# Wq and Wk as four loads of 128 whole rows, and pair 0's exponentials in two other rooms

## The chip, the cores and the metric

The kernel runs on one core of one Trainium2 chip. The metric is the device time of one execution in microseconds (us). A core has a matrix engine (PE), whose weight loads are listed as PEld, a vector engine (DVE), a scalar engine (ACT), a general engine (POOL) and a synchronizing engine (SP). Each engine runs its own list of instructions strictly in the listed order and waits at an instruction until all that it needs is there. DMA transfers are issued by SP, ACT or POOL and are carried by 16 DMA engines that all three share.

## The reference

There are 128 graphs of 128 nodes with 512 features, all in float32, and two layers:

```python
# layer 0, for each graph
h = relu(layernorm(x))
Xw = h @ Wv + bv;  sj = Xw @ aw[:512];  si = Xw @ aw[512:]
alpha = adj * exp(leaky_relu(sj[None, :] + si[:, None] + ab, 0.2))
T = alpha / (alpha.sum(-1) + 1e-12)
x = x + relu(sum over k of (T^k h) @ Wk[k] + bk[k])        # k = 0, 1, 2
# layer 1
h = relu(layernorm(x))
q, k = split(h @ Wqk);  v = h @ Wv1                        # Wqk is 512 x 1024
w = mask / sqrt(512) * rowsum(q * (adj @ (k * mask)))
x = x + softmax(w over the nodes)[:, None] * v
```

## The kernel before

The graphs are taken in 64 pairs. Both layers' products with weights are done by Strassen's scheme on 2 x 2 blocks: seven block products in place of eight, for which sums of blocks are made beforehand, of the weights once (`combine`, L205 to L211) and of the activations for each pair (`left_sums`, L407 to L410). Layer 0's weights are read as blocks b11, b12, b21, b22 (1536 columns each: three powers k), and their four sums stand in the tile `tw`, 4 x 1536 columns. Line 421 holds nearly all of PE's work.

The main loop over pairs (L596) is preceded by a setup (L557 to L588), and everything that the diff touches is in that setup:

- `norm0(0)` makes h of pair 0 and writes it to DRAM (`hd`, L310) and back in another layout (`hv`, L314), from which two DVE transposes (L320, one for each graph j of the pair) make h transposed in the tile X[0].
- `wv0_sums` multiplies the four row chunks of Wv (L133, loaded by SP) with the attention vector (L160, DVE). `attention_weights` spreads the result over the partitions by PE (L122) into `u_bc` (L168, ACT). `score_sums` (L303, DVE) then makes pair 0's scores, and `attention(0)` makes T: sums z (L353), leaky relu (L354), exponential (L356, ACT), products with the adjacency and row sums (L359), division (L361 to L365).
- `score_matrix(o)`, o = 0 to 3, makes Wq Wk^T, chunk by chunk of 128 columns of Wq and of Wk. For each o there are eight PE transposes (L236), two ACT copies (L239, L241) and the matmuls that add up in four banks (L247). Chunks 0 and 1 are loaded on ACT's queue at the start. Chunks 2 and 3 are loaded on POOL's queue into the buffers of chunks 0 and 1, so POOL waits there until PE has transposed these. A load takes 128 columns of all 512 rows, in runs of 512 bytes.
- POOL's queue also carries the blocks b for k = 1 and 2 (L202). The first of these is held behind the landing of Wv's chunk 0 by a one-column copy (L199).
- `t_transposed(0)`, `begin(0)` (the two transposes L320), `propagate(0)` (T h and T^2 h by PE, L400, copied by ACT, L402), `prepare0(0)` (the sums L407 to L410) and `combine` (L207 to L210) end the setup, followed by pair 1's norm and score sums.

The source order is not the order that the engines run. When the program is built, a scheduler takes for each engine the earliest instruction in the source that, by its own estimates of durations and of transfers, is ready. If none of a step's instructions is ready, it takes a later one. So the lists are fixed before the run. Where a tile is reused, or a region of a tile is written again, the scheduler adds the dependency, region by region. In the kernel before, z and the exponentials of pair 0 lie in `tw`, in 256 columns across the border of its first two quarters, so `combine`'s sums L207 and L209, which write these quarters, must come after T.

A transfer on SP's or ACT's queue also waits until an earlier transfer that used the same one of a few completion counters has landed.

Of the kernel before, what the change touches and what calls it, by code (L numbers as in the profile page):

```python
# [8 lines left out]
FP = mybir.dt.float32  # L9
AF = mybir.ActivationFunctionType  # L10
OP = mybir.AluOpType
# [4 lines left out]
def kernel(  # L16
# [20 lines left out]
    nc = tc.nc  # L37
    B, N, D = x.shape
    K = wk.shape[0]
    P = 128  # L40
    DC = D // P
    HC = DC // 2
    HD = D // 2
    G = 2
# [6 lines left out]
    const = ctx.enter_context(tc.tile_pool(name="const", bufs=1))  # L51
    loads = ctx.enter_context(tc.tile_pool(name="loads", bufs=3))
    front = ctx.enter_context(tc.tile_pool(name="front", bufs=2))
# [12 lines left out]
    xg, ag, agb = {}, {}, {}  # L66

    def load(p):
        load_x(p)
        load_agb(p)  # L70

    def load_x(p):
        s = slice(p * G, (p + 1) * G)
        xg[p] = loads.tile([P, G, D], FP, name="xg")
        nc.sync.dma_start(xg[p], x[s].rearrange("b n d -> n b d"))
        if p > 0:
            load_ag(p)

    def load_ag(p):
        s = slice(p * G, (p + 1) * G)  # L80
        ag[p] = loads.tile([P, G, N], FP, name="ag")
        nc.sync.dma_start(ag[p], adj[s].rearrange("b n m -> n b m"))
# [13 lines left out]


    load_x(0)
    e01 = setup.tile([P, HC, 2, HD], FP, name="e01")
    nm = setup.tile([B, N], FP, name="nm")  # L100
# [3 lines left out]
    wpool = setup_ctx.enter_context(tc.tile_pool(name="wpool", bufs=2))  # L104
    b12 = setup.tile([P, K, HC, HD], FP, name="b12")

    f = [const.tile([P, HC, 2, HD], FP, name=f"f{i}") for i in range(1, 5)]
# [5 lines left out]
    ident = const.tile([P, P], FP, name="ident")  # L113
# [7 lines left out]

        nc.tensor.transpose(dst, col.to_broadcast([P, P]), ident)  # L122

    def wqk_chunk(a, o, queue):
        w = wpool.tile([P, DC, P], FP, name=f"w{a}")
        at = a * D + o * P
        queue.dma_start(w, wqk[:, at:at + P].rearrange("(c p) o -> p c o", p=P))
        return w

    nc.scalar.dma_start(awr, aw.rearrange("n o -> o n"))  # L130
    wchunks = {0: [wqk_chunk(a, 0, nc.scalar) for a in range(2)]}
    for c in range(DC):
        nc.sync.dma_start(wv0_sb[c], wv0[c * P:(c + 1) * P])  # L133
    load_ag(0)
# [3 lines left out]
    bsum = const.tile([P, D], FP, name="bsum")  # L138
    nc.gpsimd.dma_start(bsum[:K], bk)
    nc.gpsimd.dma_start(nm, nodemask)  # L140
    wchunks[1] = [wqk_chunk(a, 1, nc.scalar) for a in range(2)]


    u_bc = const.tile([P, 2, D], FP, name="u_bc")
# [48 lines left out]
    def block0(pool, name, kh, nh):  # L193


        t = b12 if pool is None else pool.tile([P, K, HC, HD], FP, name=name)
        rows(t[:, 0], wk[0, :, nh * HD:(nh + 1) * HD], kh)
        if kh == nh == 0:
            nc.gpsimd.tensor_copy(t[:, 1, 0, 0:1], wv0_sb[0][:, 0:1])  # L199
        for k in range(1, K):  # L200
            src = wk[k, kh * HD:(kh + 1) * HD, nh * HD:(nh + 1) * HD]
            nc.gpsimd.dma_start(t[:, k], src.rearrange("(c p) o -> p c o", p=P))  # L202
        return t
# [23 lines left out]
    def score_matrix(o):  # L227

        if o == 0:
            pms.extend(ps_m.tile([P, D], FP, name="pm") for _ in range(DC))  # L230
        ws = wchunks.pop(o)
        wt = []
        for a in range(2):
            p = ps_t.tile([P, DC, P], FP, name="pt")
            for c in range(DC):
                nc.tensor.transpose(p[:, c, :], ws[a][:, c, :], ident)  # L236
            t = wpool.tile([P, D], FP, name=f"wt{a}")
            if a:
                nc.scalar.copy(t, p.rearrange("p c i -> p (c i)"))  # L239
            else:  # L240
                nc.scalar.copy(t.rearrange("p (f c a) -> p f c a", f=Q, c=DC),  # L241
                               p.rearrange("p c (f a) -> p f c a", f=Q))
            wt.append(t)
        if o + 2 < DC:
            wchunks[o + 2] = [wqk_chunk(a, o + 2, nc.gpsimd) for a in range(2)]
        for c in range(DC):
            nc.tensor.matmul(pms[c], wt[0][:, c * P:(c + 1) * P], wt[1],  # L247
                             start=(o == 0), stop=(o == DC - 1))
            if o == DC - 1:
                for nh in range(2):  # L250
                    nc.scalar.copy(e[c // HC, nh][:, c % HC, 0, :], pms[c][:, nh * HD:(nh + 1) * HD])
# [35 lines left out]
    H, HV, S, PZ, X, SX, AT, T, TT, X1, H2, X2, SX2 = ({} for _ in range(13))  # L287
# [29 lines left out]
    def transposed(hv, dst):  # L317

        for j in range(G):
            nc.vector.transpose(dst[:, j].rearrange("p f (n b) -> p f n b", n=Q),  # L320
                                hv[:, j].rearrange("p n (f a) -> p f n a", f=Q))
# [23 lines left out]
            spread(pz[:, j, :], col[:, j:j + 1])  # L345
        return pz[:, :G]

    def attention(p, room):

        a, s, pz = ag.pop(p), S.pop(p), PZ.pop(p)  # L350
        z = room.rearrange("p (g n) -> p g n", g=G)
        for j in range(G):
            nc.vector.tensor_scalar(z[:, j, :], pz[:, j, :], s[:, G + j:G + j + 1], cz, op0=OP.add, op1=OP.add)  # L353
        nc.vector.scalar_tensor_tensor(z, z, 0.2, z, op0=OP.mult, op1=OP.max)  # L354
        ex = z
        nc.scalar.activation(ex, z, AF.Exp)  # L356
        d = small.tile([P, 2, G], FP, name="d")
        for j in range(G):
            nc.vector.scalar_tensor_tensor(ex[:, j, :], ex[:, j, :], 1.0, a[:, j, :], op0=OP.mult,  # L359
                                           op1=OP.mult, accum_out=d[:, 0, j:j + 1])  # L360
        nc.vector.tensor_scalar(d[:, 0], d[:, 0], 1e-12, None, op0=OP.add)  # L361
        nc.vector.reciprocal(d[:, 1], d[:, 0])
        t = T[p] = front.tile([P, G, N], FP, name="t", bufs=1)
        for j in range(G):
            nc.vector.tensor_scalar(t[:, j, :], ex[:, j, :], d[:, 1, j:j + 1], None, op0=OP.mult)  # L365

        if p > 0:
            transposed_adj(p)

    def transposed_adj(p):  # L370

        AT[p] = front.tile([P, G, N], FP, name="aT", bufs=3)
        nc.vector.transpose(AT[p].rearrange("p g n -> p (g n)"),
                            agb.pop(p).rearrange("p g q i -> p (g q i)"))
        for j in range(G):
            b = p * G + j
            nc.scalar.activation(AT[p][:, j, :], AT[p][:, j, :], AF.Copy, scale=maskT[:, b:b + 1])

    def t_transposed(p):

        t, tt = T.pop(p), front.tile([P, G, 2, N], FP, name="tt", bufs=1)
        pt = ps_t.tile([P, DC, P], FP, name="pt")
        for j in range(G):
            nc.tensor.transpose(pt[:, j, :], t[:, j, :], ident)  # L384
        nc.scalar.copy(tt[:, :, 0, :], pt[:, :G, :])
        pt = ps_t.tile([P, DC, P], FP, name="pt")
        for j in range(G):
            nc.tensor.matmul(pt[:, j, :], t[:, j, :], tt[:, j, 0, :], start=True, stop=True)  # L388
        nc.scalar.copy(tt[:, :, 1, :], pt[:, :G, :])  # L389
        TT[p] = tt  # L390

    def propagate(p):

        h, tt = H.pop(p), TT.pop(p)
        for j in range(G):
            for kh in range(2):
                pt = ps_t.tile([P, HC, 2, N], FP, name="pt")
                for c in range(HC):
                    at = (kh * HC + c) * P
                    nc.tensor.matmul(pt[:, c].rearrange("p k n -> p (k n)"), h[:, j, at:at + P],  # L400
                                     tt[:, j].rearrange("p k n -> p (k n)"), start=True, stop=True)
                nc.scalar.copy(X[p][:, 1:3, j, kh].rearrange("p k c n -> p c k n"), pt)  # L402
# [150 lines left out]
    def begin(p):  # L553
        X[p] = front.tile([P, K, G, 2, HC, N], FP, name="x")
        transposed(HV.pop(p), X[p][:, 0].rearrange("p j h c n -> p j (h c) n"))

    norm0(0)  # L557
    wv0_sums()
    score_matrix(0)
    blocks0["b11"] = block0(const, "b11", 0, 0)  # L560
    score_matrix(1)
    attention_weights()
    masks()
    score_sums(0)
    blocks0["b12"] = block0(None, "b12", 0, 1)
    blocks0["b22"] = block0(const, "b22", 1, 1)
    load_x(1)
    blocks0["b21"] = block0(const, "b21", 1, 0)
    score_matrix(2)

    tw = const.tile([P, 4, K, HC, HD], FP, name="t")
    at = K * HC * HD - N
    attention(0, tw.rearrange("p i k c o -> p (i k c o)")[:, at:at + G * N])
    score_matrix(3)
    bias()
    t_transposed(0)
    begin(0)
    propagate(0)
    prepare0(0)
    right0.update(combine(t=[tw[:, i] for i in (0, 2, 1, 3)], **blocks0))  # L580
# [15 lines left out]
    for p in range(NP + 1):  # L596
        if p < NP:
            if p + 1 < NP:
                n = p + 1
# [19 lines left out]
        elif p > 0:  # L619
            yv, w = strassen1(p - 1, p + 2)  # L620
# [6 lines left out]
        if p < NP:  # L627
# [4 lines left out]
            else:  # L632
                transposed_by_pe(H2[p], hT2)
            a = {(j, kh): X2[p][:, j, kh:kh + 1].rearrange("p k c n -> p k (c n)")
                 for j in range(G) for kh in range(2)}
# [26 lines left out]
```

## Time and profile before

| | us |
|---|---|
| median of 6 runs | 2367.32 (2364.67 to 2370.24) |
| the profiled execution's own time | 2369.57 |
| its span on the core | 2367.8 |
| PE busy | 2341.6 (99%) |
| DVE busy | 1824.9 (77%) |
| ACT busy | 638.0 (27%) |
| POOL busy | 380.3 (16%) |

A line of the timeline gives the start, the busy time, the engine and source line, the operation, what it writes and reads, and in brackets the idle time of the engine before it with what ended it. A line of the waits gives who waited for what, then total time, count and the longest wait. A line of the windows gives a stretch of the span, its length, the busy time of each engine in it, the share of PE's full clock that was granted, the DMA share and GB/s.

### The profile page before, as it was taken

How to read it: one execution, taken by the hardware profiler on the slowest of the kernel's cores; microseconds unless marked ns; L12 is line 12 of the kernel's file. 1: busy time of each engine (PE TensorE's matmuls, PEld its weight loads, DVE VectorE, ACT ScalarE, POOL GpSimd, SP SyncE). 2: the span in 40 equal slices, each digit the busy share in tenths (PEclk: the TensorE clock that was granted, in tenths of full speed). 3: DMA queues.
4: the chain of work that ended last, by engine and by line, in shares of the span. 5: the costliest groups of instructions: out<-in, count | busy, mean ns of one | idle time of the engine just before them, and what ended most of it. 6: DMA issues, size and time to landing. Idle time of an engine off the chain costs nothing.

```text
span 2367.8 us, 27872 instructions
## 1 busy us (share of the span) xinstructions
PE 2341.6 (99%) x8929; PEld 1660.4 (70%) x8929; DVE 1824.9 (77%) x4959; ACT 638.0 (27%) x1562; POOL 380.3 (16%) x662
## 2 busy tenths in 40 slices
PE   7999999999999999999999999999999999999998
PEld 4677676676776776776766767767767667667675
DVE  6787877877877778878778778778787787787775
ACT  3222222322222222223223222222222232232221
POOL 4111111111111111111111111111111111111100
PEclk9999999999999999999999999999999999999999
DMA  7234344244343343343442443433434434424321
GB/s 209 88 97 107 97 108 106 82 117 111 85 116 106 91 107 101 104 107 89 117 106 82 116 111 86 116 104 93 107 101 104 107 89 116 107 81 116 105 63 49
DMA packets 253670, 242.88 MB, mean 103 GB/s; under 512 B 28318, under 2 KB 178846, under 8 KB 253522
## 3 DMA queue, kind: packets, MB, share of 16 engines
q1 hardware_dynamic: 228096, 211.87, 31.5%
q0 software_dynamic: 23312, 28.18, 6.4%
q8 instruction: 70, 1.15, 0.2%
q10 hardware_dynamic: 2114, 1.05, 0.2%
q14 instruction: 78, 0.64, 0.1%
HBM read 140.72 MB, written 100.27 MB: 102 GB/s over the span
## 4 chain that ended last, share of the span: by engine, by line
PE 90%; DVE 3%; DMA 2%; issue 1%; ACT 0%; POOL 0%; DVEq 0%; POOLq 0%
PE pm L421 76%; PE pt L400 8%; PE pt L519 4%; PE pt L388 1%; DMA pwd<-pwt 1%; PE pt L384 1%; DMA pw<-pwd 0%; DVE st L260 0%; DMA pz<-pzd 0%; DMA pzd<-pzt 0%; DVE x L549 0%; DVE x L461 0%; DVE x L320 0%; DVE junk L303 0%; DVE sx L409 0%
## 5 line engine op out<-in xcount | busy, mean ns | idle before, releaser
L421 PE MATMUL pm<-t,sx 128*128 128x256 f32 x2304 | 508.0, 379 | 2.9 <-DVE sx L408 2.9
L421 PEld LDWEIGHTS pm<-t,sx 128*128 128x128 f32 x2304 | 437.5, 190 | 63.0 <-DVE sx L408 3.5
L421 PE MATMUL pm<-b,x 128*128 128x256 f32 x1536 | 363.1, 379 | 0.0
L421 PE MATMUL pm<-f,sx 128*128 128x512 f32 x768 | 352.4, 594 | 1.4 <-DVE s L479 1.3
L421 PEld LDWEIGHTS pm<-b,x 128*128 128x128 f32 x1536 | 282.2, 190 | 59.7 <-issue 29.7
L339 POOL DMA_DIRECT2D pzd<-pzt x124 | 69.1, 559 | 1410.7 <-DVE pzt L336 1410.6
L421 PEld LDWEIGHTS pm<-f,sx 128*128 128x128 f32 x768 | 145.8, 191 | 185.7 <-issue 161.9
L402 ACT COPY x<-pt 128x512 f32<-128x512 f32 x256 | 147.6, 576 | 370.4 <-PE pt L400 370.2
L421 PE MATMUL pm<-e,x 128*128 128x512 f32 x512 | 242.5, 596 | 3.1 <-DVE x L320 3.1
L400 PE MATMUL pt<-tt,h 128*128 128x256 f32 x1024 | 231.6, 379 | 0.5 <-ACT tt L389 0.5
L303 DVE SCALAR_TENSOR_TENSOR junk<-h,u_bc 128x512 f32<-128x512 f32 x256 | 177.1, 692 | 64.1 <-ACT h L278 52.9
L400 PEld LDWEIGHTS pt<-tt,h 128*128 128x128 f32 x1024 | 194.5, 190 | 27.5 <-ACT tt L389 1.1
L421 PE MATMUL pm<-b,sx 128*128 128x256 f32 x768 | 176.2, 379 | 0.0
L421 PE MATMUL pm<-t,x 128*128 128x256 f32 x768 | 176.2, 379 | 0.0
L320 DVE STREAM_TRANSPOSE x<-hv 128x512 f32<-128x512 f32 x254 | 165.0, 688 | 9.7 <-DMA hv<-hd 9.1
L421 PEld LDWEIGHTS pm<-e,x 128*128 128x128 f32 x512 | 97.7, 191 | 99.6 <-issue 91.0
L356 ACT ACTIVATE s<-s 128x256 f32<-128x256 f32 x63 | 26.3, 417 | 514.3 <-DVE s L354 514.3
L421 PEld LDWEIGHTS pm<-b,sx 128*128 128x128 f32 x768 | 145.9, 190 | 19.8
L421 PEld LDWEIGHTS pm<-t,x 128*128 128x128 f32 x768 | 145.9, 190 | 19.8
L92 POOL DMA_DIRECT2D agb<-in_adj_dram x256 | 153.3, 603 | 23.3 <-issue 13.3
L278 ACT ACTIVATE h<-xg,rs 128x512 f32<-128x512 f32 x128 | 97.4, 807 | 170.3 <-DVE rs L272 170.3
L519 PE MATMUL pt<-h,aT 128*128 128x512 f32 x256 | 130.7, 592 | 0.0
(145 smaller groups left out, 2814.3 us busy)
## 6 DMA issues: line engine op xcount, KB each, us to landing
hd<-h SPq DMA_DIRECT2D x127, 512.0 KB, 3.8
hv<-hd SPq DMA_DIRECT2D x508, 128.0 KB, 5.2
xg<-in_x_dram SPq DMA_DIRECT2D x64, 512.0 KB, 3.6
out_dram<-x SPq DMA_DIRECT2D x63, 512.0 KB, 2.8
ag<-in_adj_dram SPq DMA_DIRECT2D x64, 128.0 KB, 2.6
agb<-in_adj_dram POOLq DMA_DIRECT2D x256, 32.0 KB, 3.7
pw<-pwd POOLq DMA_DIRECT2D x63, 128.0 KB, 3.3
pz<-pzd POOLq DMA_DIRECT2D x62, 128.0 KB, 5.2
```

What stands on the lines that cost most here:

```text
L92: nc.gpsimd.dma_start(agb[p][c * S32:(c + 1) * S32].rearrange("p g q i -> p (g q) i"), v[c])
L278: nc.scalar.activation(to, at, AF.Relu, bias=rs[:, 1, j:j + 1], scale=rs[:, 0, j:j + 1])
L303: nc.vector.scalar_tensor_tensor(junk, h[:, j, :], 1.0, u_bc[:, a, :], op0=OP.mult, op1=OP.mult, accum_out=s[:, a * G + j:a * G + j + 1])
L320: nc.vector.transpose(dst[:, j].rearrange("p f (n b) -> p f n b", n=Q), hv[:, j].rearrange("p n (f a) -> p f n a", f=Q))
L339: nc.gpsimd.dma_start(d[j], t[j::S32])
L356: nc.scalar.activation(ex, z, AF.Exp)
L384: nc.tensor.transpose(pt[:, j, :], t[:, j, :], ident)
L388: nc.tensor.matmul(pt[:, j, :], t[:, j, :], tt[:, j, 0, :], start=True, stop=True)
L400: nc.tensor.matmul(pt[:, c].rearrange("p k n -> p (k n)"), h[:, j, at:at + P], tt[:, j].rearrange("p k n -> p (k n)"), start=True, stop=True)
L402: nc.scalar.copy(X[p][:, 1:3, j, kh].rearrange("p k c n -> p c k n"), pt)
L421: nc.tensor.matmul(bank[:, :r.shape[-1]], left[i][:, k, c * P:(c + 1) * P], r, start=(first and at == 0), stop=(at == len(chunks) - 1), sk ...
L519: nc.tensor.matmul(to, AT[p][:, j, :], h2, start=True, stop=True)
```

## The change

The eight loads of Wq and Wk by columns become four loads by rows: each brings 128 whole rows (4096 bytes each) on ACT's queue at the start. They lie in `tw`, one in each quarter (columns 0 to 1023 of the first, 512 to 1535 of the others), until `combine` overwrites them. POOL's four loads of chunks 2 and 3 go. Pair 0's z moves to the tile `junk`. Its exponentials move to two rooms of 128 columns: graph 0's to the last block of X[0]'s part for h transposed, which the transpose of graph 1 writes, and graph 1's to `tw` across the border of the first two quarters. The single exponential over 256 columns becomes two over 128. `begin(0)` is written out, as X[0] is allocated earlier. The load of pair 1's x gets a one-column copy from `u_bc` ahead of it. All other pairs keep their code.

```diff
-    def load_x(p):
+    def load_x(p, gate=None):
...
+        if gate is not None:
+            nc.scalar.copy(xg[p][:, 0, 0:1], gate)
         nc.sync.dma_start(xg[p], x[s].rearrange("b n d -> n b d"))
...
-    def wqk_chunk(a, o, queue):
-        w = wpool.tile([P, DC, P], FP, name=f"w{a}")
-        at = a * D + o * P
-        queue.dma_start(w, wqk[:, at:at + P].rearrange("(c p) o -> p c o", p=P))
-        return w
+    tw = const.tile([P, 4, K, HC, HD], FP, name="t")
+    wqk_sb = [tw[:, c].rearrange("p k c o -> p (k c o)")[:, D * (c > 0):][:, :2 * D] for c in range(DC)]
     nc.scalar.dma_start(awr, aw.rearrange("n o -> o n"))
-    wchunks = {0: [wqk_chunk(a, 0, nc.scalar) for a in range(2)]}
+    for c in range(DC):
+        nc.scalar.dma_start(wqk_sb[c], wqk[c * P:(c + 1) * P])
...
-    wchunks[1] = [wqk_chunk(a, 1, nc.scalar) for a in range(2)]
...
-                nc.tensor.transpose(p[:, c, :], ws[a][:, c, :], ident)
+                nc.tensor.transpose(p[:, c, :], wqk_sb[c][:, a * D + o * P:a * D + (o + 1) * P], ident)
...
-        if o + 2 < DC:
-            wchunks[o + 2] = [wqk_chunk(a, o + 2, nc.gpsimd) for a in range(2)]
...
-    def attention(p, room):
+    def attention(p, room, rooms=None):
...
-        ex = z
-        nc.scalar.activation(ex, z, AF.Exp)
+        if rooms is None:
+            ex = [z[:, j, :] for j in range(G)]
+            nc.scalar.activation(z, z, AF.Exp)
+        else:
+            ex = rooms
+            for j in range(G):
+                nc.scalar.activation(ex[j], z[:, j, :], AF.Exp)
...
-    load_x(1)
+    load_x(1, u_bc[:, 1, 0:1])
...
-    tw = const.tile([P, 4, K, HC, HD], FP, name="t")
-    at = K * HC * HD - N
-    attention(0, tw.rearrange("p i k c o -> p (i k c o)")[:, at:at + G * N])
+    X[0] = front.tile([P, K, G, 2, HC, N], FP, name="x")
+    at = K * HC * HD - N // 2
+    attention(0, front.tile([P, D], FP, name="junk", bufs=1)[:, :G * N],
+              [X[0][:, 0, 1, 1, HC - 1], tw.rearrange("p i k c o -> p (i k c o)")[:, at:at + N]])
...
-    begin(0)
+    transposed(HV.pop(0), X[0][:, 0].rearrange("p j h c n -> p j (h c) n"))
```

## The prediction

> **What bounds the kernel now.** I read the windows first. Their columns are the stretch, its length, busy time of PE, PEld, DVE, ACT and POOL, PE's granted clock, the DMA share and GB/s.
>
> ```profile
> 12.00:25.00 13.00, 12.11 (x42) 7.14 (x43) 3.84 (x14) 3.31 (x7) 8.11 (x12) 1.00 0.94 256
> 25.00:31.00 6.00, 5.98 (x27) 3.54 (x28) 2.70 (x8) 1.66 (x3) 0.00 (x0) 1.00 1.07 289
> 31.00:34.00 3.00, 1.29 (x3) 0.47 (x3) 2.32 (x9) 1.33 (x3) 0.00 (x0) 0.94 0.95 235
> 34.00:39.00 5.00, 5.00 (x10) 2.00 (x10) 4.96 (x6) 1.99 (x7) 0.00 (x0) 0.70 0.75 205
> 89.00:99.00 10.00, 6.85 (x11) 3.03 (x11) 9.45 (x29) 1.37 (x3) 0.00 (x0) 0.66 0.17 58
> 100.00:2300.00 2200.00, 2197.93 (x8428) 1568.01 (x8427) 1721.77 (x4699) 597.64 (x1470) 350.33 (x602) 1.00 0.38 102
> ```
>
> From 100 to 2300 us PE is busy 2197.93 of 2200: a change in the setup gives nothing there and can only move all of it earlier or later. In the setup PE loses time at two places, 31 to 34 (1.29 busy of 3) and 34 to 39, where it is always busy but at 0.70 of its clock. The DMA engines are full from 12 to 31 us. Next, the waits up to 60 us, PE's and DVE's:
>
> ```profile
> PE pt L236 <- DMA w<-in_L_gnn_Wqk_dram: 3.7, 1, 3.7
> PE pm L421 <- DVE sx L408: 2.0, 1, 2.0
> PE pm L247 <- ACT wt L239: 1.7, 1, 1.7
> ```
> ```profile
> DVE cz L176 <- PE pt L175: 8.9, 1, 8.9
> DVE x L320 <- DMA hv<-hd: 3.8, 1, 3.8
> ```
>
> The timeline from 27 us shows that the second and third of PE's waits begin in DVE's wait for hv:
>
> ```profile
> 27.04 0.73 DVE L353 TENSOR_SCALAR t<-pt,col,cz 128x128 f32<-128x128 f32 x2
> 31.62 0.71 DVE L320 STREAM_TRANSPOSE x<-hv 128x512 f32<-128x512 f32 x1 [3.85 <-DMA hv<-hd]
> 32.25 0.38 DVE L354 SCALAR_TENSOR_TENSOR t<-t 128x256 f32<-128x256 f32 x1
> 32.55 0.70 DVE L320 STREAM_TRANSPOSE x<-hv 128x512 f32<-128x512 f32 x1
> 32.67 0.42 ACT L356 ACTIVATE t<-t 128x256 f32<-128x256 f32 x1 [5.17 <-DVE t L354]
> 32.99 0.57 ACT L239 COPY wt<-pt 128x512 f32<-128x512 f32 x1
> 33.61 0.50 PEld L247 LDWEIGHTS pm<-wt,wt 128*128 128x128 f32 x2 [2.53 <-ACT wt L239]
> 34.09 0.48 DVE L365 TENSOR_SCALAR t<-t,d 128x128 f32<-128x128 f32 x2
> 34.50 1.76 DVE L207 TENSOR_TENSOR t<-b,b 128x1536 f32<-128x1536 f32 x1
> ```
>
> z is ready at 27.77, but a transpose of h stands next in DVE's list and its data lands at 31.6. The leaky relu, the exponential and, on ACT behind the exponential, the last copy of score_matrix(3) all wait for it; PE waits for that copy.
>
> **The change part by part.** Sums are against the profiled execution, 2369.57 us (span 2367.8 and 1.8 around it, which the change doesn't touch); it lies 2.25 above the median of the runs, so the change is carried over to 2367.32.
>
> *T ahead of the transposes.* From L354 (32.25) to the end of L365 (34.57) is 2.32 us. Started at 27.8, T ends at 30.1. The second exponential adds about 0.2: an ACT row of 128 x 128 (L183) takes 0.31, so two make 0.62 against 0.42. T then ends at 30.3, against 34.57. The transposes of score_matrix(3) run from 30.37, its copies (0.59 each) end near 32.0, and PE is busy with the bias until 31.91: PE's wait goes, **-1.7**. The slow clock of 34 to 39 follows directly on this wait: at a mean of 0.70, 1.5 of 5 us are lost, and with 0.94 from 31 to 34 another 0.2. I take it to go with the wait: **-1.7** (bounds -1.7 and 0). Against this the Trainium skill speaks ("TensorE: Matmul & The Clock Gate", Part 1): the clock falls after an idle window of about 3.4 us. The idle here was 1.71, about half a window, so by the page alone the fall need not be this wait's and could stay; the sum would then be 1.7 less good.
>
> *DVE's chain.* DVE is busy 4.96 of 5 us to 39 and 3.98 of 4 before PE's sx wait at 48.9, so it is nearly the path. Behind T come two transposes (0.7 each), four weight sums (1.75 each, 7.0 in all, ended at 41.86) and then pair 1's statistics, whose relu on ACT and score sums (0.69 each) stand between left sums L407 and L408. With 3.85 of idle gone, the weight sums end near 38.0 while X's copies come 3.4 earlier, and pair 1's steps start ahead of them. The sx wait of 2.0 shrinks: bounds 0 and -2.0; I take **-1.5**, nearer to the far end because the two score sums and the relu behind it (2 x 0.69 + 0.8) are all that filled it. What is late next is ACT's copies of X (0.59 each, behind PE).
>
> *The loads.* Eight loads of 256 KB become four of 512 KB, 2.1 MB as before. No row shows 4096-byte runs on ACT's queue; the nearest are Wv's 256 KB on SP (6.5 us to landing, median), the old w on ACT (8.3) and x's 512 KB (3.6). Every o now needs all four loads, where the first needed two. PE's first big wait ended at 12.1 with w. Lower bound for the last of the four: aw, x and Wqk alone are 2.6 MB, at 289 GB/s 9 us after the first issue at 0.7, thus about 10. Upper bound: with Wv and the eight POOL blocks (2.1 MB) wholly ahead of it 5.8 MB, 20 us, thus about 20.7. POOL's four removed issues (0.76 each, 3.0) and its 7.7 us of waits for L236 held those blocks until 14.4; now they can start when Wv's chunk 0 has landed and the one-column copy is done, some 7 us. So the edit that frees POOL also takes away what kept it out of Wqk's way. I take 13.0, nearer the first bound, since the blocks join only when much of Wqk is under way. A page of the skill speaks against this change and my value ("DMA: Bandwidth & Descriptors", "Issuing engines are not separate DMA queues"): loads issued by ACT, SP and POOL interleave on the same 16 engines. By it alone Wqk could land with the blocks at the upper bound, 7.7 later, and the sum would be +2.8. After w's landing PE took 2.8 to its first L247 (14.97) with 12 transposes to do (3.03 us); of the 16 now needed, three quarters can be done as their rows land, leaving four (1.0) and two copies (1.2). So L247 starts at 15.2 and I take **0.0**; each further us of landing costs 1 on PE, until hv or DVE is later. hv, behind less traffic at its end, should land before 31.5; that is not priced.
>
> *Small things at nothing.* The copy ahead of pair 1's x (some 0.2 on ACT) lies in ACT's 7.5 us before u_bc. Behind that load on SP are pair 1's adjacency and b21's rows; in the trace they were issued at 25.7 to 32.4, u_bc was ready at 24.3, so the gate opens in time; if u_bc slips 5 us, xg's landing (34.6, first used 39.5) still has cover. z in `junk` only follows the score sums, on the same engine. `combine` now also waits for the last transposes L236 (30.8), and T covers that within 0.5. Pair 2's loss at 89 to 99 (3.15 idle and a clock of 0.66) is a chain of its own through POOL and should shift with the rest; it could change by 3 either way, kept for the range.
>
> Sum: -1.7 - 1.7 - 1.5 + 0.0 = -4.9. The execution would be 2364.7, the median **2362.4**.
>
> **The rivals.** 0.2% of this kernel, about what a measurement can tell from no change, is 4.7 us.
>
> *Wqk late (within 0.2%).* The blocks from POOL crowd Wqk and the last load lands at 15 to 17. For it: DMA share 0.94 to 1.07 from 12 on, so every byte moved forward pushes another back. PE's L247 starts 2 to 4 us late and eats most of 4.9: 2364 to 2367. A variant is that the change doesn't do what it says: graph 0's exponentials lie in the part of X[0] that the transpose of graph 1 writes, so graph 0's transpose is free to stay between L353 and L354. Then the stall lasts until hv lands, and only an earlier hv helps; with hv at 31.5 the time is 2367.
>
> *A transpose ahead of the score sums (slower).* DVE has 8.9 us of idle before cz. Graph 0's transpose needs no room of T's. If the scheduler's estimate of hv, now on a queue with other neighbours, falls into that idle, the transpose is listed before L303. On the chip hv lands at up to 31.5, and behind it then stand four score sums (3.0), the spreads and z (1.5), and T (2.5): T ends at 39.2 rather than 34.57, +4.7, and PE's list has its last score matrix behind ACT's exponential as before. That gives 2372. It decides from an hv landing after about 27; against it speaks that hv's issue at 17 waits for h and its round trip to DRAM, which the list's estimate knows.
>
> **How the numbers follow.** The forecast case, faster by over 0.2%, gets 0.47: the stall's cause is in the trace and needs only order, but the sum passes 4.7 barely, with room to go to 2357 if hv also lands early, u_bc comes ahead of the score matrices and pair 2's loss shrinks. Within 0.2%: 0.33, Wqk late or graph 0's transpose left where it was. Slower: 0.20, of which 0.12 for the transpose ahead of the score sums and 0.08 for a changed list in the 62 equal pairs, where 0.1 us each makes 6. The range runs from 2357 to 2371.5. The forecast case alone would be 2357 to 2362.6.
>
> **What would show it.** Right: L354 directly behind L353 and ahead of L320; no wait of L247 on L239; clock 1.00 from 31 to 39; no w on POOL; L202 issued from about 7; PE's 24 to 48 us matmuls 3 to 5 us earlier, and the same 3.15 us wait of pair 2, earlier by the same. Wrong: L236 waiting for Wqk after 15 us, DVE waiting for hv ahead of L354 or L303, or a PE busy share below 99.9% from 100 to 2300.

## The result: slower by 0.3%, and the profile after

The changed kernel takes 2371.88 us in the median (2369.77 to 2376.04, 18 runs), the kernel before 2364.90 us on the same chips (2360.91 to 2370.24, 38 runs). The ratio is 1.0030, 95% interval 1.0024 to 1.0036: **7.0 us slower**, where 4.9 less was forecast. (The six runs that the forecast started from had 2367.32 in the median; it is the difference that is compared.) The profiled execution took 2370.71 us, its span is 2368.9.

Line numbers have moved a little: the transposes L236 are now L235, score-matrix matmuls L247 are L244, z is L351 (was L353), the leaky relu L352 (L354), T's last step L368 (L365), the matmuls of T h L403 (L400), the loads of Wq and Wk L132 (L127). The windows of the changed kernel, with the columns as before (busy time of PE, PEld, DVE, ACT, POOL, granted clock, DMA share, GB/s):

```profile
12.00:25.00 13.00, 6.58 (x18) 4.04 (x19) 5.87 (x25) 4.73 (x10) 1.15 (x2) 1.00 0.97 293
31.00:34.00 3.00, 2.27 (x21) 2.07 (x20) 1.85 (x6) 1.92 (x6) 0.00 (x0) 1.00 0.09 14
34.00:39.00 5.00, 4.99 (x19) 2.54 (x18) 4.15 (x16) 1.98 (x6) 0.00 (x0) 1.00 0.81 264
89.00:99.00 10.00, 6.72 (x18) 3.68 (x17) 7.60 (x24) 1.00 (x2) 0.00 (x0) 0.83 0.12 26
100.00:2300.00 2200.00, 2198.60 (x8428) 1566.91 (x8427) 1723.47 (x4698) 597.03 (x1469) 350.23 (x602) 1.00 0.39 102
```

The two losses that the change was aimed at are gone: from 34 to 39 PE has the full clock (0.70 before), and it keeps it from 25.74 to 94.01. These two windows hold other work now, as everything here is some 8 us later; the surer sign is that PE has no wait for a copy ahead of a matmul of the score matrix (L244) any more, in the whole setup. But a larger hole has opened ahead of them: from 12 to 25 us PE is busy 6.58 of 13, where it was 12.11. The DMA engines are not the idle ones there: they move 293 GB/s, before 256. Behind 100 us nothing is lost. The waits up to 60 us, of PE, of DVE and of ACT (engine, what it waited for: us in total, times, longest), say who holds the hole:

```profile
PE pt L235 <- DMA t<-in_L_gnn_Wqk_dram: 11.0, 4, 4.0
PE pm L424 <- DVE sx L411: 1.2, 1, 1.2
```
```profile
DVE cz L176 <- PE pt L175: 13.3, 1, 13.3
DVE junk L160 <- ACT f L156: 6.3, 1, 6.3
```
```profile
ACT r L262 <- DMA f<-in_L_gnn_Wv_dram: 9.9, 1, 9.9
```

PE now waits at every one of the four loads, 11.0 us in all (3.7 before). DVE no longer waits for hv, but waits 13.3 us for PE's spread. And ACT, whose list had no such wait before, computes nothing for 9.9 us. ACT's own rows of the timeline show why (start, duration, engine, line; ACTq is ACT's issuing of transfers; the second and third row come from narrower views of the same timeline and are the last two of the four issues of the first row):

```profile
1.32 10.56 ACTq L132 DMA_DIRECT2D t<-in_L_gnn_Wqk_dram  x4
7.23 0.33 ACTq L132 DMA_DIRECT2D t<-in_L_gnn_Wqk_dram  x1
11.54 0.33 ACTq L132 DMA_DIRECT2D t<-in_L_gnn_Wqk_dram  x1
11.92 0.30 ACT L262 ACTIVATE r<-mv,eps 128x2 f32<-128x2 f32 x1 [9.90 <-DMA f<-in_L_gnn_Wv_dram]
20.87 0.59 ACT L240 COPY wt<-pt 128x512 f32<-128x512 f32 x1 [7.60 <-PE pt L235]
22.79 1.54 ACT L275 ACTIVATE h<-xg,rs 128x512 f32<-128x512 f32 x2
```

ACT has four loads to issue ahead of its first computation. Two go out at once. The third goes out at 7.23, directly behind the landing of Wv's chunk 0 (7.21), the fourth at 11.54, behind that of Wv's chunk 2 (11.52): by the trace's semaphore records each uses the same completion counter as that chunk. Before, the third and fourth shared the counters of x (landed 4.85) and of Wv's chunk 0 (5.50), went out at 4.87 and 5.52, and cost ACT nothing, since its first activation needed DVE's statistics until 6.41 anyway. Now that activation runs at 11.92, and the four loads land at 6.78, 10.60, 15.55 and 20.32. Behind it ACT stands still once more, for 7.60 us: the copies of the first score matrices come next in its list and wait for PE's transposes of the late rows, and h, which stands behind them, is made at 22.79 instead of 7.96. So ACT's own delay was over well before the last rows landed; what PE waited for is the late loads. What follows on PE and DVE:

```profile
22.00 4.26 PE L244 MATMUL pm<-wt,wt 128*128 128x512 f32 x5
25.57 5.40 PE L244 MATMUL pm<-wt,wt 128*128 128x512 f32 x12
35.20 0.73 DVE L351 TENSOR_SCALAR junk<-pt,col,cz 128x128 f32<-128x128 f32 x2
35.96 0.42 DVE L352 SCALAR_TENSOR_TENSOR junk<-junk 128x256 f32<-128x256 f32 x1
37.91 0.28 DVE L368 TENSOR_SCALAR t<-t,d 128x128 f32<-128x128 f32 x1
```

The score matrix starts at 22.00 (14.97 before, +7.0). Its first matmuls are 0.85 apart, those from 25.57 on 0.45: PE, idle for most of the stretch before, has only half its clock until 25.74 (until 16.54 before). This is read from the spacing: the profile's record of the clock begins with its first rise, so the 1.00 of the rows from 12 to 25 says nothing about the time ahead of it. At half clock for 3.7 us of score matrix instead of 1.6 it loses some 1 us more (an estimate), and z comes at 35.20 (27.04, +8.2). From z on the order is the one that the change was after: the leaky relu directly behind z, T complete at 38.2, both transposes later. The first matmul of T h stands at 45.69, before at 41.18: +4.5.

### The profile page after: what moved, and what is told of

Same layout as the page of the kernel before. It is cut to its first block, busy times and chain, and to the rows that moved or that the text cites. A ratio compares the mean times of both kernels' runs of the same rounds, so it can differ in the third digit from the quotient of the medians.

```text
span 2368.9 us, 27862 instructions
## 1 busy us (share of the span) xinstructions
PE 2340.9 (99%) x8929; PEld 1658.8 (70%) x8929; DVE 1824.6 (77%) x4959; ACT 637.2 (27%) x1564; POOL 377.2 (16%) x658
## 4 chain that ended last, share of the span: by engine, by line
PE 92%; DVE 2%; DMA 1%; issue 1%; ACT 0%; POOL 0%; DVEq 0%; POOLq 0%; ACTq 0%
PE pm L424 77%; PE pt L403 9%; PE pt L522 4%; PE pt L391 1%; DMA pwd<-pwt 1%; PE pt L387 1%; DMA pz<-pzd 0%; DMA pw<-pwd 0%; DMA pzd<-pzt 0%; DVE x L552 0%; DVE st L257 0%; DVE x L464 0%; DVE x L317 0%; DVE sx L412 0%; ACT ej L542 0%
## 5 line engine op out<-in xcount | busy, mean ns | idle before, releaser
L403 PE MATMUL pt<-tt,h 128*128 128x256 f32 x1024 | 231.6, 379 | 0.5 <-ACT tt L392 0.5
L403 PEld LDWEIGHTS pt<-tt,h 128*128 128x128 f32 x1024 | 194.5, 190 | 27.5 <-ACT tt L392 1.1
L317 DVE STREAM_TRANSPOSE x<-hv 128x512 f32<-128x512 f32 x254 | 165.0, 688 | 4.7 <-DMA hv<-hd 3.7
L355 ACT ACTIVATE s<-s 128x256 f32<-128x256 f32 x63 | 26.3, 417 | 517.1 <-DVE s L352 517.1
```

The lines of the kernel that those rows point to most:

```text
L355: nc.scalar.activation(z, z, AF.Exp)
```

## The experiments

The questions: which part of the +7.0 is the loads' and which the rooms'; whether the late Wq and Wk come from ACT's issues being held by their counters, or from POOL's blocks, which now run beside them; and what removing the stall is worth by itself. "Before" is measured on the same chip each time. The stages come from one profile each (us): landing of the last of the four row loads of Wq and Wk (left empty where they are loaded by columns), first matmul of the score matrix, z, first matmul of T h, and the time between the last two.

| kernel | median | before | ratio (95%) | last load | score matrix | z | T h | z to T h |
|---|---|---|---|---|---|---|---|---|
| before, profiled | | | | | 14.97 | 27.04 | 41.18 | 14.1 |
| before_again | one run, 2368.72 | 2364.81 | | | 14.68 | 26.47 | 42.56 | 16.1 |
| before_third | one run, 2364.63 | 2364.81 | | | 15.21 | 26.89 | 37.95 | 11.1 |
| after | 2371.88 | 2364.90 | 1.0030 (1.0024 to 1.0036) | 20.32 | 22.00 | 35.20 | 45.69 | 10.5 |
| after_again | one run, 2375.74 | 2365.28 | | 20.26 | 21.95 | 34.56 | 45.06 | 10.5 |
| loads_alone | 2373.38 | 2364.67 | 1.0031 (1.0020 to 1.0043) | 20.64 | 22.33 | 35.90 | 46.59 | 10.7 |
| rooms_alone | 2366.01 | 2364.67 | 1.0006 (0.9998 to 1.0015) | | 14.45 | 32.19 | 43.16 | 11.0 |
| blocks_late | 2370.35 | 2364.67 | 1.0020 (1.0011 to 1.0029) | 17.49 | 19.17 | 32.69 | 43.19 | 10.5 |
| two_on_sp | 2367.37 | 2364.67 | 1.0011 (1.0002 to 1.0020) | 12.38 | 15.50 | 29.07 | 37.47 | 8.4 |
| both | 2366.12 | 2364.81 | 1.0007 (0.9998 to 1.0016) | 13.44 | 16.74 | 28.82 | 38.88 | 10.1 |
| both_across | 2367.64 | 2365.28 | 1.0010 (1.0001 to 1.0018) | 12.28 | 15.57 | 28.12 | 38.60 | 10.5 |
| rooms_across | 2364.29 | 2365.28 | 0.9995 (0.9986 to 1.0003) | | 15.03 | 27.74 | 38.24 | 10.5 |
| rooms_across_2 | 2363.35 | 2366.03 | 0.9986 (0.9977 to 0.9995) | | 14.81 | 27.70 | 38.19 | 10.5 |

### The two parts apart

**loads_alone**: the new loads with before's rooms.

```diff
-    load_x(1, u_bc[:, 1, 0:1])
+    load_x(1)
...
-    X[0] = front.tile([P, K, G, 2, HC, N], FP, name="x")
-    at = K * HC * HD - N // 2
-    attention(0, front.tile([P, D], FP, name="junk", bufs=1)[:, :G * N],
-              [X[0][:, 0, 1, 1, HC - 1], tw.rearrange("p i k c o -> p (i k c o)")[:, at:at + N]])
+    at = K * HC * HD - N
+    attention(0, tw.rearrange("p i k c o -> p (i k c o)")[:, at:at + G * N])
...
-    transposed(HV.pop(0), X[0][:, 0].rearrange("p j h c n -> p j (h c) n"))
+    begin(0)
```

> The changed kernel's four loads by rows with the kernel before's rooms, its begin(0) and no copy ahead of pair 1's x. My theory (the loss comes with the loads: ACT stands behind its third and fourth load until 11.9 us, the last rows of Wqk land at about 20 us and PE's first score matrix starts near 22 instead of 15): the first L400 matmul of propagate(0) near 45 to 47 us of the span and 5 to 10 us slower than before. The rival, that the rooms and the copy cost it: within 2 us of before, with T late only in the other kernel.

Measured: 1.0031, all of the loss. The loads land as in the changed kernel and the score matrix starts at 22.33. DVE's waits up to 60 us show one thing more:

```profile
DVE st L257 <- DMA xg<-in_x_dram: 12.2, 2, 8.1
```

Without the gate pair 1's statistics stand ahead of pair 0's scores in DVE's list, and DVE waits 8.1 us there for pair 1's x (it takes the place of most of the wait for cz, of which 3.8 is left, so it lies in the same hole). The loads alone explain the loss. And from z on this kernel, which has before's rooms, also has T ahead of the transposes (L352 is the leaky relu, L317 the transposes):

```profile
36.66 0.42 DVE L352 SCALAR_TENSOR_TENSOR t<-t 128x256 f32<-128x256 f32 x1
42.83 1.30 DVE L317 STREAM_TRANSPOSE x<-hv 128x512 f32<-128x512 f32 x2
```

From z to T h it takes 10.7 us, as the changed kernel does.

**rooms_alone**: before's loads, and the other half of the change.

```diff
-    load_x(1)
+    load_x(1, u_bc[:, 1, 0:1])
...
-    at = K * HC * HD - N
-    attention(0, tw.rearrange("p i k c o -> p (i k c o)")[:, at:at + G * N])
+    X[0] = front.tile([P, K, G, 2, HC, N], FP, name="x")
+    at = K * HC * HD - N // 2
+    attention(0, front.tile([P, D], FP, name="junk", bufs=1)[:, :G * N],
+              [X[0][:, 0, 1, 1, HC - 1], tw.rearrange("p i k c o -> p (i k c o)")[:, at:at + N]])
...
-    begin(0)
+    transposed(HV.pop(0), X[0][:, 0].rearrange("p j h c n -> p j (h c) n"))
```

> The kernel before's loads with the changed kernel's rooms, the copy ahead of pair 1's x and begin written out. My theory: no loss of 7 us here; graph 0's transpose stands ahead of z in DVE's list, so DVE waits for hv until about 31.5 us as in the kernel before, and the time is -1 to +2 us of before. The rival, that the rooms carry the loss: 5 us or more slower.

Measured: 1.0006, no clear difference. The rooms are then innocent of the loss, but they do not bring the gain either. Its timeline at the place of the stall (L322 is the transpose, L355 z, L249 the score matrix here):

```profile
31.55 0.71 DVE L322 STREAM_TRANSPOSE x<-hv 128x512 f32<-128x512 f32 x1 [4.81 <-DMA ag<-in_adj_dram]
32.19 0.69 DVE L355 TENSOR_SCALAR junk<-pt,col,cz 128x128 f32<-128x128 f32 x2
34.40 1.22 PE L249 MATMUL pm<-wt,wt 128*128 128x512 f32 x1 [2.88 <-ACT wt L241]
```

One transpose, graph 0's, now stands even ahead of z, and DVE stands there 4.81 us until the last of hv lands (31.43; the row names another transfer of that moment). PE's wait for the copy is 2.88 us instead of 1.71, and half clock follows from 33.38 to 40.20. Of the two rooms one lies in graph 1's half of X[0], so only graph 1's transpose is bound to come after T. In the changed kernel both are listed behind T, but in loads_alone they are too, without these rooms. Over the kernels with either of these two sets of rooms the order goes with the time of h: where h is made at 20 to 23 us (the changed kernel, loads_alone, blocks_late) both transposes stand behind T, and where it is made near 8 (before, rooms_alone, two_on_sp, both) at least one stands ahead of T. So these rooms don't decide it. That the scheduler's estimate of hv's landing is the link was not tried by itself.

### Why Wq and Wk land late

**blocks_late**: the changed kernel, but POOL's blocks for k = 1 and 2 wait for the last load of Wq and Wk.

```diff
-        if kh == nh == 0:
-            nc.gpsimd.tensor_copy(t[:, 1, 0, 0:1], wv0_sb[0][:, 0:1])
+        nc.gpsimd.tensor_copy(t[:, 1:3, 0, 0], wqk_sb[DC - 1][:, 0:2])
```

> The changed kernel with the eight blocks of layer 0's weights on POOL's queue held by a copy from the last of the four row loads instead of one from Wv's first chunk. If the blocks crowd Wqk out (my theory's second part): the last rows land near 15 to 16 us instead of 20.3, PE's first score matrix starts near 17.5 and 3 to 5 us of the 7 come back (2367 to 2369). If only ACT's held issues count: landing above 18.5, gain below 1.5 us.

Measured: 2370.35, ratio 1.0020, by the medians 1.3 of the 7.0 us less. That is between the two expectations, and as the intervals of the two ratios overlap, the times alone don't show a gain. The trace shows the landing move: with the blocks out of the way the first loads land only 0.5 us earlier (6.26, 10.07), the last two at 15.09 and 17.49 instead of 15.55 and 20.32. The waits up to 60 us of PE and of ACT:

```profile
PE pt L234 <- DMA t<-in_L_gnn_Wqk_dram: 8.2, 4, 4.1
```
```profile
ACT r L261 <- DMA f<-in_L_gnn_Wv_dram: 9.8, 1, 9.8
```

ACT's wait of 9.8 us has not moved: it does not come from POOL's blocks. The score matrix still starts 4.2 us later than in before's first profile (19.17 against 14.97).

**two_on_sp**: the changed kernel, but the third and fourth load are issued by SP, behind x and ahead of Wv. The code of POOL's blocks stays as in the change.

```diff
-    for c in range(DC):
+    for c in range(2):
         nc.scalar.dma_start(wqk_sb[c], wqk[c * P:(c + 1) * P])
+    for c in range(2, DC):
+        nc.sync.dma_start(wqk_sb[c], wqk[c * P:(c + 1) * P])
```

> The changed kernel with the third and fourth row load issued by SP behind pair 0's x and ahead of Wv; ACT issues two and goes on. If the held issues on ACT matter (my theory's first part): h is made near 9.5 us instead of 24.3, hd is issued near 13 instead of 24.4, the last rows land near 14 to 16 us, and the time is 3 to 8 us below the changed kernel, near or below the one before. If only the blocks' traffic counts: landing still near 20 us and a gain below 2 us.

Measured: 2367.37, ratio 1.0011, 4.3 of the 7.0 us less. All four loads have gone out by 2.2 us and the last lands at 12.38. ACT's rows:

```profile
6.04 0.29 ACT L264 ACTIVATE r<-mv,eps 128x2 f32<-128x2 f32 x1 [4.02 <-DVE mv L260]
7.59 1.52 ACT L277 ACTIVATE h<-xg,rs 128x512 f32<-128x512 f32 x2 [0.55 <-DVE rs L271]
```

The first activation is back at 6.04 and h at 7.59. The score matrix starts at 15.50, T h at 37.47: 8.2 us earlier than in the changed kernel and 3.1 earlier than the mean of before's three profiles (40.6).

But the edit moves more than the two issues. POOL's blocks are held by Wv's chunk 0, and this now lands behind Wq and Wk, at 12.87. POOL's rows here:

```profile
12.92 0.18 POOL L201 COPY b<-f 128x1 f32<-128x1 f32 x1 [7.84 <-DMA f<-in_L_gnn_Wv_dram]
13.04 5.75 POOL L204 DMA_DIRECT2D b<-in_L_gnn_Wk_dram  x8
```

In the changed kernel the same eight went out from 7.38. So this kernel is rid of both causes at once, the held issues and the blocks' traffic, and its 4.3 us are the worth of both. What the held issues cost is seen against blocks_late, where the blocks also come behind the last load (from 18.63): the last load lands 5.1 us earlier here, the score matrix starts 3.7 earlier and the time is 3.0 us less on the same chip (95% interval 0.9 to 4.9, from resampling the 11 runs of each). In this difference lies also that the two loads now go ahead of Wv, and that the blocks follow 5.6 us sooner; these were not tried apart.

The time does not follow all the way: PE then waits 2.7 us for pair 1's sums of X at 67 to 70, and half clock follows from 69.90 for 3.41 us.

**both**: both edits.

The two diffs above, together.

> The changed kernel with two row loads on SP ahead of Wv and the eight blocks held by the landing of the last row load. If the held issues on ACT and the blocks' traffic are the whole loss of the loads: last rows at 12 to 14 us, PE's first score matrix at 14 to 15, the time 1 to 3 us below the kernel with two loads on SP (2364 to 2366), no better than before by more than 2. If the loss lies elsewhere: no different from the kernel with two loads on SP, 2367.

Measured: 2366.12, ratio 1.0007, 5.7 of the 7.0 us less. This is nearly two_on_sp once more: the blocks go out from 13.52 instead of 13.04, and the last load lands no earlier (13.44 against 12.38). The 1.4 us between the two is within their intervals, and it can't be added up as the blocks' share. Here too something is taken back later. Its window from 67 to 74 and its wait in that stretch:

```profile
67.00:74.00 7.00, 4.28 (x15) 3.27 (x14) 6.71 (x22) 2.93 (x7) 0.00 (x0) 0.84 0.00 0
```
```profile
PE pm L425 <- DVE sx L412: 2.7, 1, 2.7
```

Before was busy 6.02 of these 7 us at full clock. Here DVE makes three sums of layer 1's weights from 63.30 to 66.8 ahead of pair 1's sums of X.

### What the removed stall is worth

**before_again** and **before_third**: the kernel before, profiled twice more.

> The kernel before, unchanged: a second profile of it, since its first was of an execution of 2369.57 us where the median of its runs is near 2364.7. If my theory holds that the profiled execution stands for all: DVE waits 3 to 4 us for hv near 31 us, PE waits 1.7 us ahead of the last score matrix and its clock falls. The rival, that this execution's setup or pair 2's wait was an unlucky one: a span 3 to 5 us shorter, with the difference in one place, most likely the clock's fall in the setup or near 90 us.

> The kernel before once more, a third profile. The same two expectations: the waits near 31 to 34 us as in the first profile, or a shorter span with one of the slow clock stretches (33.6 to 37.0 and 91.6 to 98.5 us in the first) absent or shorter.

Measured: the loss that the prediction was to remove is not the same in each execution. The windows from 34 to 39 us, of before_again and of before_third:

```profile
34.00:39.00 5.00, 5.00 (x6) 2.00 (x7) 4.93 (x7) 1.54 (x5) 0.00 (x0) 0.50 0.86 227
```
```profile
34.00:39.00 5.00, 4.54 (x20) 2.86 (x19) 5.00 (x5) 2.59 (x8) 0.00 (x0) 1.00 0.66 174
```

PE's wait for the copy was 1.71, 2.47 and 0.31 us in the three profiles, with hv's last part landing at 31.49, 31.70 and 29.94. Behind the first two the clock fell for 3.41 and 6.83 us, behind the third it didn't. There it fell at 46.71, behind a wait at 43 to 47.

**rooms_across**: before's loads, the gate, and graph 0's exponentials laid across the border of the two halves of X[0], so that neither transpose may come before T. Against rooms_alone:

```diff
-              [X[0][:, 0, 1, 1, HC - 1], tw.rearrange("p i k c o -> p (i k c o)")[:, at:at + N]])
+              [X[0][:, 0].rearrange("p g h c n -> p (g h c n)")[:, D - N // 2:D + N // 2],
+               tw.rearrange("p i k c o -> p (i k c o)")[:, at:at + N]])
```

> The kernel before's loads, with graph 0's exponentials in 128 columns across the border of the two parts of X[0] that the two transposes of h write, so that both transposes must come after T. It is the prediction's first step by itself. If that step was right: DVE doesn't wait for hv ahead of T, PE doesn't wait for the last copy of score_matrix(3), the clock stays up from 31 to 39 us, propagate(0)'s first matmul is near 37.5 us, and the time is 1 to 4 us below before (2361 to 2364). If the wait only moves on, to the transposes themselves or to pair 1's left sums: within 1 us of before.

Measured: 2364.29 against 2365.28, ratio 0.9995, not clear of 1. But the mechanism is there in full. The windows of this kernel, and then two rows of its timeline:

```profile
34.00:39.00 5.00, 4.54 (x19) 2.71 (x18) 5.00 (x4) 2.75 (x9) 0.00 (x0) 1.00 0.70 205
89.00:99.00 10.00, 9.76 (x36) 5.95 (x35) 9.74 (x31) 5.23 (x13) 0.00 (x0) 1.00 0.18 54
```
```profile
27.74 0.73 DVE L355 TENSOR_SCALAR junk<-pt,col,cz 128x128 f32<-128x128 f32 x2
30.65 1.30 DVE L322 STREAM_TRANSPOSE x<-hv 128x512 f32<-128x512 f32 x2
```

z at 27.74, T done by 30.7, then both transposes without a wait; no wait of PE on the copy, and full clock from 17.5 us to 2355.6 of 2360.2. T h starts at 38.24.

**rooms_across_2**: the same kernel on another chip, for its sign.

> The same kernel as rooms_across, for its sign: there the median lay 1.0 us below before's, ratio 0.9995 with 0.9986 to 1.0003. If the stall's removal is worth in the median what it is worth in the mean of three profiles of before (the first left sums at 40.6 there against 38.2), this gives 2362.5 to 2364 again, some 1 to 2.4 us below before. If what is gained in the setup is lost again behind it, this gives 2364.5 to 2366, ratio 0.9998 to 1.0004. A gain of 4.9, as the prediction had it, would be 2360.

Measured: 2363.35 against 2366.03, ratio 0.9986, interval 0.9977 to 0.9995: faster, and the profile repeats the stages within 0.25 us. Over both chips the gain is 1.0 and 2.7 us, about the 2.4 by which T h starts earlier than in the mean of before's three profiles. This is the one version that beats the kernel before, by 0.05 to 0.14% (the first ratio isn't clear of 1 by itself); it loads Wq and Wk as before did.

**both_across**: `both` with the rooms of rooms_across (that diff on top of the other two).

> The kernel with two loads on SP and the blocks held, with graph 0's exponentials across the border as well, so that both transposes come after T. If graph 0's transpose ahead of z costs that kernel something when hv is late: 1 to 2 us below it (2364 to 2365). If not: the same as it, 2366.

Measured: 1.0010. The stages are those of rooms_across within 0.6 us until T h (38.60), but pair 1's wait of 2.7 us at 68 stays, and the median isn't below that of `both`. Against rooms_across on the same chip it is 3.4 us slower: the loads by rows bring nothing even when they land early.

**after_again**: the changed kernel, profiled once more.

> The changed kernel, unchanged: a second profile. If its loss lies in the setup and is the same in every execution: the last rows of Wqk at 20 to 21 us, propagate(0)'s first matmul near 45 to 46, as in the first profile. If it varies with the landing of the loads as the kernel before's does: more than 2 us away from that.

Measured: the setup repeats (last load 20.26, score matrix 21.95, T h 45.06), and the single time is 2375.74.

## Why the prediction was wrong, point by point

- **The loads, taken at 0.0: this is the step that failed.** It took the last landing at 13.0 and the score matrix at 15.2; the trace has 20.3 and 22.0, so the term was +7.0. (That each further us of landing costs 1 on PE was right: 7.3 and 7.0.) The landing fell on the upper bound that the working had set (20.7), but only in part for its reason. That bound let Wv and POOL's eight blocks go ahead of Wq and Wk; holding these blocks back alone brings the landing to 17.5, and 1.3 us of time that are not clear of the noise. The larger part, from 17.5 to 12.4 and 3.0 us of time, is one that the working left out. It counted the bytes of four loads from a first issue at 0.7, as if all four went out then, but not that an issue may wait for an earlier transfer's counter: the third went out at 7.23 and the fourth at 11.54. Together the two parts give back 4.3 of the 7.0 us (two_on_sp). The trace of before showed such waits, with ACT's third issue at 4.87 and its fourth at 5.52, where they cost nothing. The change altered the sequence of transfers, and with it which landing each issue waits for.
- **The Trainium skill's rule against the change.** "DMA: Bandwidth & Descriptors" ("Issuing engines are not separate DMA queues") says that loads issued by several engines interleave on the same 16 engines. The runs agree: blocks_late lands the last load 2.8 us earlier. The prediction weighed it for 7.7 us and then passed it over for 13.0. The number of the page's side was nearer, but this traffic accounts for the smaller part, 2.8 us of the 7.9 between 20.3 and 12.4; that the larger number fitted is luck.
- **T ahead of the transposes, -1.7 and -1.7: the size came out, but in the changed kernel not by the rooms.** From z to T h the profile of before took 14.1 us, the changed kernel takes 10.5 in both of its profiles. That is 3.6 less, where 3.4 was forecast, and the reason why z comes 8.2 us later but T h only 4.5. But loads_alone takes 10.7 with before's rooms, and rooms_alone leaves a transpose ahead of z with the new ones. The order that was forecast came with the late loads, so the agreement is luck. That the step itself holds, T first and with it no wait and no fall of the clock, is shown by rooms_across, where the rooms force it: 10.5 in both profiles.
- **The same, carried to the median: too large.** In three profiles of before the stretch took 14.1, 16.1 and 11.1, with hv's last part landing between 29.9 and 31.7. rooms_across isolates the gain: 1.0 and 2.7 us in the median. That is below the 3.4 of these two terms, and further below the 4.9 of the whole sum. Against the 10.5 of rooms_across the stall costs 3.6, 5.6 and 0.6 us of this stretch in the three (before_third has hardly any wait there and loses its clock at 46.71 instead of at 33.6), and a part is taken back: from 60 to 80 us PE is busy 19.02 of 20 us in all three profiles of before, 18.40 in both of rooms_across.
- **PE's sx wait, -1.5**: it went from 2.0 to 1.2, so -0.8, though behind a later start.
- **The first rival, Wqk late**, named the right place, but only the smaller of the two causes and too small a price: it took 15 to 17 for the landing and let the gain pay for it. Its variant, graph 0's transpose left where it was, is real in rooms_alone, two_on_sp and both, where it is listed even ahead of z; in the changed kernel both transposes are listed behind T. **The slower rival**, a transpose ahead of the score sums, didn't occur in any of these profiles. The slower result came by late loads, the first rival's place, not through this one.
- **Small things at nothing**: right. Pair 2's wait is 3.3 (3.1 before), and 100 to 2300 us is as busy as it was.

What is left open: T h starts 4.8 us later in the mean of two profiles of the changed kernel than in the mean of three of before, and the median time is 7.0 larger. A part of that may lie in which executions were profiled: before's three lie 2.7 us above its median on average, the changed kernel's two 1.3. From T h to the end these two take 2323 and 2329 us, and all thirteen profiles lie between 2322 and 2329 without a clear order by kernel, so a single profile can't say where the other 2 us are.

## What to carry to other kernels

Before transfers are regrouped, list what every issue waits for and what stands behind it on its engine: a changed sequence of transfers changes which landing an issue is tied to, so that a load can go out much later than its place in the list suggests, and on an engine that also computes the work behind it is held as well (9.9 us of ACT here). After an experiment, look in its trace for what else the edit has moved: two_on_sp was to move two issues and moved POOL's blocks too. A stall of an engine that runs 0.3 to 2.5 us long from one execution to the next is to be priced by several profiles, not by the one at hand. And when an edit has two parts, price and try them apart: here one part, with its rooms laid right, was worth 1 to 3 us, and the other cost 7 to 9 by itself.

## What the runs showed of the hardware

- The clock's changes lie on a grid of 3.413 us in each profile: before has full clock from 16.543 for 17.067 (5 x 3.413), half for 3.413 from 33.610. Laid over the thirteen profiles up to 200 us, all 13 grid stretches at full clock in which PE was idle for 1.97 us or more were followed by half clock. Of the eleven with 1.43 to 1.95 three were followed by half clock (1.43, 1.70 and 1.85, all of them the wait for the copy, which stands directly behind the bias matmuls on 3 rows) and eight were not, and below 1.43 none was. The Trainium skill ("TensorE: Matmul & The Clock Gate", Part 1) gives a window of about 3.4 us, which agrees with the grid, and a fall after an idle window; the runs differ in that the window needn't be idle throughout. Why 1.43 sufficed once and 1.95 another time didn't, was not tried.
- A load of 512 KB in runs of 4096 bytes took 5.5 to 8.9 us from issue to landing in the changed kernel; the fourth, issued at 11.54 beside POOL's blocks, took 8.8, and with these held back 6.1.
